# Masked attention with a residual: features in plain order, one store per quadrant, other slots for the blocks of batches five and six

## The chip, the cores and the metric

One core of a Trainium2 chip. The time is device microseconds of one execution, the median of several. Engines: PE (TensorE, matmul), DVE (VectorE), ACT (ScalarE), POOL (GpSimd) and SP (SyncE); SP, POOL and ACT also issue the transfers (DMAs), each through a queue of its own, and 16 DMA engines carry them out.

## What is computed

Eight batches of x, 512 features by 1024 tokens, float32, and a mask of zeros and ones with about half of the tokens kept. Queries, keys and values are one projection; 8 heads of 64 features.

```python
def reference(x, cond_2048, Wq, Wo):        # x (8, 512, 1024), mask (8, 1024), W (512, 512)
    q = transpose(x) @ Wq.T                  # split into 8 heads of 64
    scores = einsum('bhqd,bhkd->bhqk', qh, qh) / sqrt(64)
    logits = (scores * cmask + (1 - cmask) * -1e30) * rmask
    ctx = softmax(logits) @ qh               # heads joined again
    return x + transpose(ctx @ Wo.T)
```

A row whose token is masked has logits of zero throughout, so its attention is the mean of all values.

## The kernel before

Attention is computed for the kept tokens only (NK = 544 columns hold them, the last one the mean of x, which stands for every masked token). `early` runs before the number of kept tokens is known to the engines, `late` after a branch on it.

**Order of features.** A [128, 512] tile of x or of a weight has four features per partition or column group. Here partition p holds features 4p to 4p + 3: `load_piece` (L369) loads half a batch (512 tokens) as four transfers, one for each d, whose DRAM side has 128 rows with equal steps (L376). The rows of x that are written back to DRAM for the gather (`turn`, L399, stored by SP at L413; for batch 0 `turn_first`, L380) thus have columns in an order (a, d, f) other than the features'. `order_columns` (L926) and the wo branch of `turn_weights` (L938) bring the weights into it, `by_rows` and `as_rows` (L797) the last batch's results, and the stores at the end undo it.

**One batch** is four pairs of heads, and a pair five steps c = 0 to 4; `late` walks through 8 x 4 x 5 steps. In a step, PE computes scores (L610) and weighted values (L655), ACT the exponentials (L633). `project`, `turn_values` and `square` prepare the next pair. At a pair's step 0 `invert` (L727) turns the sums of the pair before: DVE writes rt, SP stores it in four small transfers (row, L736) and reads it back spread over partitions in two (rb, L741); at step 3 `contexts` (L756) uses rb on DVE (`sum_last`, L751). DVE works in order, so what stands behind a wait there, such as the copy of v (L545) that PE needs, waits too.

**Around it**, `plan` (L1087) puts tasks into steps by (batch, pair, step) with a rank. Tasks of rank below 5 come before `contexts`, the others behind it. For batch n: `load_piece` in batch n-2 at (0,1) and (0,2), the rows' transposes, the search for kept tokens on DVE, the gather on POOL (L474) and `collect`. For the results of batch b:

- `output` (L770): PE multiplies by wo (L780), ACT copies, POOL stores the rows into od (L793).
- `load_rows` (L846): SP loads 128 rows of x into a block g, 32 tokens of each quarter of the batch, in four transfers (L850). `firsts` has the steps.
- `fetch` (L888): POOL adds the results to g with an indirect transfer. `slots` has the steps.
- `finish_blocks` (L853): DVE transposes g into the buffer whole (L857), of which there is one. `ends` has the steps. After the last block (batches 0 to 4) or each fourth (5 and 6) a store is queued, which `issue_stores` (L910) issues at the end of the next step but one at most: 16 transfers on SP (L867), for each of four token quarters (a) and four feature groups (c).

Batch 7 has no pair after it to hide in. `begin_output` (L803) multiplies the first three pairs' part during the last pair, `end_output` adds the rest, `fetch_last` gathers by token, `finish_tokens` (L897) transposes back on PE, adds the x tile that still lies in SBUF, and ACT stores (L906).

SP, POOL and ACT issue transfers in program order; a transfer on SP waits for the one eight before it.

Of the kernel before, what the change touches and what calls it, by code (L numbers as in the profile page):

```python
# [10 lines left out]
F32 = mybir.dt.float32  # L11
# [10 lines left out]
Q = 32  # L22
# [283 lines left out]
def attention_of_kept_tokens(ctx, tc, x, mask, wq, wo, out, ident, wqT, woT, verdict, flag):  # L306


    nc = tc.nc
    B, D, T = x.shape  # L310
    P = 128
    DK = D // NH
    SCALE = 1.0 / math.sqrt(DK)
    ND = D // P
# [52 lines left out]
    stores = [[], []]  # L367

    def load_piece(b, r, queue=None):  # L369

        features = x[b].rearrange("(p d) t -> d p t", d=ND)
        if r == 0:
            xs[b] = []
        xs[b].append(sb.tile([P, ND, NB], F32, tag="x", name=f"x_{b}_{r}", bufs=NN))
        for d in range(ND):
            (queue or nc.sync).dma_start(  # L376
                xs[b][r][:, d, :], features[d][..., r * NB : (r + 1) * NB]
            )
# [417 lines left out]

    def by_rows(pr):  # L797
        return woT[:, pr, :].rearrange("p (a d f) -> p d a f", a=A, d=ND)

    def as_rows(t):  # L800
        return t.rearrange("p (d a f) -> p d a f", a=A, d=ND)

    def begin_output(b, i):  # L803

        n = sizes[i]
        po = bank(f"pa_{b}_{i}")
        for pr in range(ND - 1):
            nc.tensor.matmul(  # L808
                as_rows(po[:n, :]),
                cTs[b, pr][:, i * P : i * P + n],  # L810
                by_rows(pr),
                start=(pr == 0),
                stop=(pr == ND - 2),
            )
        pa = sb.tile([P, D], F32, tag="xin", name=f"pa_{b}_{i}", bufs=NC)
        note(nc.scalar.copy(pa[:n, :], po[:n, :]))
        partials[i] = pa

    def end_output(b, i, tag):
        n = sizes[i]  # L820
        od = place_outputs(b)
        po = bank(f"po_{b}_{i}", tag)
        nc.tensor.matmul(
            as_rows(po[:n, :]),
            cTs[b, ND - 1][:, i * P : i * P + n],
            by_rows(ND - 1),
            start=True,
            stop=True,
        )
# [12 lines left out]

    def by_blocks(t):
        return t.rearrange("(c f d) (a n) -> a f c d n", c=A, d=ND, a=A)

    def load_rows(b, i):  # L846
        g = sb.tile([P, D], F32, tag="g", name=f"g_{b}_{i}", bufs=NT)
        rows = rows_of_x[b][:T, :].rearrange("(a n) c -> a n c", a=A)
        for a in range(A):
            nc.sync.dma_start(g[a * Q : (a + 1) * Q, :], rows[a, i * Q : (i + 1) * Q, :])  # L850
        gs[b, i] = g

    def finish_blocks(b, i):  # L853
# [7 lines left out]
        if (i + 1) % n == 0:  # L861
            cols = slice((i + 1 - n) * Q, (i + 1) * Q)

            def store():
                for a in range(A):
                    for c in range(A):
                        nc.sync.dma_start(  # L867
                            by_blocks(out[b])[a][:, c, :, cols],
                            whole[a * Q : (a + 1) * Q, c * ND : (c + 1) * ND, cols],
                        )  # L870

# [25 lines left out]
    def finish_tokens(b, i):  # L897
# [4 lines left out]
        for d in range(ND):  # L902
# [3 lines left out]
        nc.scalar.dma_start(  # L906
            out[b, :, i * P : (i + 1) * P].rearrange("(p d) t -> p d t", d=ND), xr
        )
# [16 lines left out]

    def order_columns(w, nm):  # L926

        ws = []
        for e in range(ND):
            t = sb.tile([P, D], F32, tag="g", name=f"{nm}_in_order_{e}", bufs=NT)  # L930
            nc.scalar.copy(
                t.rearrange("p (a d f) -> p a d f", a=A, d=ND),
                w[e].rearrange("p (a f d) -> p a d f", a=A, d=ND),
            )
            ws.append(t)
        return ws

    def turn_weights(wT, nm, d, tag="t"):  # L938
        pt = bank(f"{nm}_t{d}", tag)
        for e in range(ND):  # L940
            nc.tensor.transpose(
                pt[:, e * P : (e + 1) * P], weights[nm][e][:, d * P : (d + 1) * P], ident
            )
        if nm == "wo":
            nc.scalar.copy(
                wT[:, d, :].rearrange("p (a d f) -> p a d f", a=A, d=ND),
                pt.rearrange("p (a f d) -> p a d f", a=A, d=ND),
            )
        else:
            nc.scalar.copy(wT[:, d, :], pt)  # L950

    def early():
# [64 lines left out]
        for r in range(NN):  # L1017
# [10 lines left out]
            nc.scalar.copy(searches[0][0][:, r * NB : (r + 1) * NB], pt)  # L1028
            if r == 0:
                for i in range(NT):  # L1030
                    turn_first(i)

# [15 lines left out]

        mean_first()
        for i in range(NC):  # L1050
            search(0, i)

    def count_blanks():
# [33 lines left out]
    def plan():  # L1087
# [62 lines left out]
        for b in range(B - 1):  # L1150
            nxt = b + 1
            if b < B - 3:
# [7 lines left out]
                firsts, slots = after[3:], after[6:]  # L1160
                ends = [(1, 4), (2, 0), (2, 1), (2, 4), (3, 0), (3, 0), (3, 1), (3, 4)]
                ends = [(nxt + 1, *at) for at in ends]
            elif b == B - 3:
                for i in range(LAST - 1):
                    put(nxt, i + 1, 3, output, b, i, 0, rank=6)
                    put(nxt, i + 1, 4, output, b, i, 1, rank=6)
                put(nxt, 3, 2, output, b, LAST - 1, 0, 1, rank=6)
                put(nxt, 3, 2, output, b, LAST, 0, 1, rank=6)
                firsts = [(nxt, 3, i) for i in range(NC)] + [(nxt + 1, 0, i) for i in range(NT - NC)]
                slots = [(nxt + 1, 0, (i + 1) // 2) for i in range(NT)]  # L1170
                ends = [(0, 3), (0, 4), (1, 0), (1, 1), (1, 1), (1, 2), (1, 4), (2, 0)]
                ends = [(nxt + 1, *at) for at in ends]
            else:
                put(nxt, 0, 4, output, b, 0, 0, 1, rank=6)
                put(nxt, 1, 2, output, b, LAST, 0, 1, rank=6)
                put(nxt, 1, 3, output, b, 1, 0, 1, rank=6)
                put(nxt, 1, 4, output, b, 2, 0, 1, rank=6)
                put(nxt, 2, 3, output, b, 3, 0, 1, rank=6)
# [22 lines left out]
    def late(n):  # L1201
# [176 lines left out]
```

## Time and profile before

| | |
|---|---|
| median of 3 runs | 764.5 us (753.38, 764.5, 764.69) |
| the profiled execution | 761.91 us |
| its span | 760.2 us |
| mean granted clock of PE | 0.929 |
| moved by DMA | 116.75 MB, 154 GB/s on average |

The span runs from the first to the last instruction of the profiled execution. In a line of the profile's timeline stand start, length (both us), engine, line of the kernel, operation and the tiles written and read, then how many instructions were merged; a bracket tells how long the engine had stood idle before and what ended that. SPq, POOLq and ACTq are those engines' issuing of transfers. In a line of the windows stand the stretch, its length, the busy time of PE, PEld (weight load), DVE, ACT and POOL, the clock, the DMA engines' busy share and GB/s.

### The profile page before, as it was taken

The page shows a single profiled execution, that of the slowest core. Times are in us where ns is not written, and L with a number is a line of the kernel's source. Part 1 is how long each engine was busy: PE and PEld are TensorE (multiplying, and loading weights), DVE is VectorE, ACT ScalarE, POOL GpSimd, SP SyncE. Part 2 cuts the span into 40 slices and gives each one's busy share as a digit, 9 for nine tenths or more (in the row PEclk, how much of TensorE's full clock was granted, in tenths as well). Part 3 has the DMA queues.
Part 4 walks back from the last instruction along what each step waited for, and adds up shares of the span by engine and source line. Part 5 has one row for each costly group of instructions (what it writes and reads, how often), then busy time and mean ns, then how long its engine had stood idle before and what let it go on. Part 6 is the DMA issues. An engine that isn't in the chain of part 4 may idle for free.

```text
span 760.2 us, 16407 instructions
## 1 busy us (share of the span) xinstructions
PE 650.5 (86%) x6187; PEld 368.8 (49%) x6187; DVE 347.8 (46%) x1044; ACT 375.1 (49%) x1048; POOL 183.1 (24%) x205
## 2 busy tenths in 40 slices
PE   5588899999999999799979997999999919989630
PEld 4454555555555554455535554555555505543220
DVE  7227566544545562455445552465445214332420
ACT  5365376666556654456535654655544504453000
POOL 4601302001243122412142121412241421133210
PEclk9788799999999999899989999999999968999855
DMA  8626535223677467863977387854773484455282
GB/s 279 219 63 191 154 95 170 72 88 92 207 167 183 106 184 211 180 166 105 273 171 165 91 234 207 187 143 124 195 159 88 108 199 111 130 126 97 93 259 49
DMA packets 100372, 116.75 MB, mean 154 GB/s; under 512 B 15488, under 2 KB 67200, under 8 KB 100272
## 3 DMA queue, kind: packets, MB, share of 16 engines
q1 hardware_dynamic: 79360, 74.09, 34.6%
q0 software_dynamic: 16688, 39.32, 22.3%
q10 hardware_dynamic: 4224, 2.10, 0.9%
q8 instruction: 52, 0.85, 0.5%
q14 instruction: 48, 0.39, 0.2%
HBM read 72.78 MB, written 42.67 MB: 152 GB/s over the span
## 4 chain that ended last, share of the span: by engine, by line
PE 51%; DMA 15%; SPq 14%; DVE 10%; issue 3%; ACT 3%; POOL 1%; POOLq 0%; DVEq 0%; ACTq 0%
PE pq L517 12%; PE s L610 11%; PE av L655 10%; PE po L780 8%; SPq L867 6%; SPq L850 4%; DMA rb<-row 4%; DMA g<-xd 4%; DMA row<-rt 3%; DMA x<-in_x_dram 3%; PE v L543 2%; PE pa L808 2%; DVE v L545 1%; SPq L741 1%; SPq L736 1%
## 5 line engine op out<-in xcount | busy, mean ns | idle before, releaser
L633 ACT ACTIVATE e<-s,bias 128x544 f32<-128x544 f32 x256 | 180.2, 709 | 107.7 <-PE s L610 107.5
L655 PE MATMUL av<-e,v 64*64 64x272 f32 x2048 | 152.8, 401 | 34.5 <-DVE v L545 34.3
L610 PE MATMUL s<-qT 64*64 64x272 f32 x2048 | 152.1, 410 | 0.0
L517 PE MATMUL pq<-xc,wqT 128*128 128x273 f32 (+1 forms) x512 | 138.1, 413 | 0.4 <-ACT wqT L950 0.4
L889 POOL DMA_INDIRECT g<-od,block_origin x56 | 88.4, 1578 | 144.4 <-DMA g<-xd 83.9
L655 PEld LDWEIGHTS av<-e,v 64*64 64x64 f32 x2048 | 79.8, 137 | 78.8 <-DVE v L545 38.5
L780 PE MATMUL po<-woT,cT 128*128 128x512 f32 (+1 forms) x448 | 115.9, 443 | 0.0
L517 PEld LDWEIGHTS pq<-xc,wqT 128*128 128x128 f32 x512 | 94.2, 194 | 43.8 <-issue 25.9
L610 PEld LDWEIGHTS s<-qT 64*64 64x64 f32 x2048 | 68.2, 135 | 69.7 <-issue 44.7
L793 POOL DMA_DIRECT2D od<-oc x56 | 30.7, 551 | 205.8 <-ACT oc L791 198.0
L474 POOL DMA_INDIRECT xin<-xd,source x40 | 38.0, 950 | 156.3 <-DMA row<-rt 42.8
L531 DVE COPY qm<-pq 128x1 f32<-128x1 f32 x32 | 5.1, 158 | 150.0 <-ACT qT L526 134.9
L780 PEld LDWEIGHTS po<-woT,cT 128*128 128x128 f32 (+1 forms) x448 | 48.3, 159 | 32.5 <-issue 31.7
L552 ACT ACTIVATE sq<-v 128x640 f32<-128x640 f32 x32 | 23.5, 736 | 59.3 <-DVE v L545 59.3
L545 DVE COPY v<-v 128x512 f32<-128x512 f32 x64 | 31.1, 487 | 47.2 <-PE v L543 47.2
L524 ACT COPY qT<-pq 128x272 f32<-128x272 f32 x64 | 24.7, 385 | 56.1 <-PE pq L517 56.1
L633 ACT ACTIVATION_READ_ACCUMULATOR e<-s,bias 128x1 f32 x256 | 50.1, 196 | 0.0
L857 DVE STREAM_TRANSPOSE whole<-g 128x512 f32<-128x512 f32 x56 | 38.0, 691 | 26.2 <-DMA g<-xd 16.2
L405 DVE STREAM_TRANSPOSE xt<-x 128x1024 f32<-128x1024 f32 x28 | 34.6, 1236 | 15.3 <-DMA x<-in_x_dram 14.6
L464 DVE TENSOR_SCALAR_CACHE_REDUCE junk<-rank,key 128x1024 f32<-128x1024 f32 (+4 forms) x40 | 39.9, 997 | 1.1 <-ACT rank L1028 1.1
L558 DVE TENSOR_REDUCE len<-sq 128x10 f32<-128x640 f32 x32 | 26.2, 820 | 27.3 <-ACT sq L552 27.3
L633 ACT ACTIVATE el<-s,bias 128x272 f32<-128x272 f32 x64 | 30.3, 478 | 12.5 <-PE s L624 12.3
(148 smaller groups left out, 605.0 us busy)
## 6 DMA issues: line engine op xcount, KB each, us to landing
x<-in_x_dram SPq DMA_DIRECT2D x56, 256.0 KB
xd<-xt SPq DMA_DIRECT2D x112, 128.0 KB
g<-xd SPq DMA_DIRECT2D x224, 64.0 KB
out_dram<-whole SPq DMA_DIRECT2D x80, 128.0 KB
rb<-row SPq DMA_DIRECT2D x60, 160.0 KB
od<-oc POOLq DMA_DIRECT2D x28, 256.0 KB, 2.5
out_dram<-whole SPq DMA_DIRECT2D x64, 64.0 KB
rank<-ranks SPq DMA_DIRECT2D x6, 512.0 KB
```

The source lines that it names most:

```text
L405: nc.vector.transpose(xt.rearrange("p k (d f) -> p k d f", d=ND), xs[b][r][:, :, at : at + n].rearrange("p d (k t) -> p k d t", t=Q),)
L464: nc.vector.tensor_scalar(junk[:, :n], rank[:, i * P :], key[:, col], 0.0, ALU.is_le, ALU.add, accum_out=found[:, col])
L474: nc.gpsimd.indirect_dma_start(out=xin[:n, :], out_offset=None, in_=rows_of_x[b], in_offset=bass.IndirectOffsetOnAxis(ap=searches[b][2][:n ...
L517: nc.tensor.matmul(pq[:, :n], wqT[:, d, pr * P : (pr + 1) * P], xcs[b][:, d, hf * KH : hf * KH + n], start=(d == 0), stop=(d == ND - 1),)
L545: nc.vector.tensor_copy(v[:, at : at + n, :], pt[:, : n * P].rearrange("p (c d) -> p c d", d=P))
L610: nc.tensor.matmul(s[h][to, hf, :KH], qT[heads[h], at : at + DK], qT[heads[h], hf * KH : (hf + 1) * KH], start=True, stop=True,)
L633: nc.scalar.activation(e[:, h], of[h], AF.Exp, bias=biases[pair][:, c : c + 1], scale=SCALE, accum_out=acc[:, h, c : c + 1],)
L655: mm = nc.tensor.matmul(avs[pair][hf][heads[h], :KH], v[rows, c, heads[h]], e[rows, h, hf, :] if c < LAST else e[rows, h, :], start=(c == ...
L780: nc.tensor.matmul(po[j * n : (j + 1) * n, :w], cTs[b, pr][:, i * P : i * P + n], woT[:, pr, j * w : (j + 1) * w], start=(pr == 0), stop=( ...
L857: nc.vector.transpose(whole[:, :, i * Q : (i + 1) * Q], gs.pop((b, i)).rearrange("p (k f) -> p k f", f=Q))
L867: nc.sync.dma_start(by_blocks(out[b])[a][:, c, :, cols], whole[a * Q : (a + 1) * Q, c * ND : (c + 1) * ND, cols],)
L889: nc.gpsimd.indirect_dma_start(out=gs[b, i], out_offset=None, in_=ods[b], in_offset=bass.IndirectOffsetOnAxis(ap=block_origin[:, b, i : i ...
```

## The change

Feature a·128 + d·32 + f now sits in partition a·32 + f under index d, so rows of x, weights and results have columns in the features' own order. `order_columns`, `by_rows`, `as_rows` and the wo branch go. A block's rows of x are loaded in one transfer, a quadrant (a) of results is stored in one. `finish_tokens` writes features d·128 + p, for which the last batch's x is loaded a second time (`load_again`, two transfers of 1 MB at steps 1 and 2 of that batch). At the start, `turn_first` comes behind both halves of the ranks and `mean_first` behind the search. In `plan`, the last end of batches 0 to 4 is three steps earlier; outputs, loads, fetches and ends of batches 5 and 6 (counted from 0) have other steps, and `begin_output` of the short last block moves behind the last pair's sums.

```diff
+    def load_again(b, r):
+        if r == 0:
+            xs[b] = []
+        xs[b].append(sb.tile([P, ND, NB], F32, tag="x", name=f"xe_{b}_{r}", bufs=NN))
+        nc.sync.dma_start(
+            xs[b][r], x[b, :, r * NB : (r + 1) * NB].rearrange("(d p) t -> p d t", d=ND)
+        )
...
-        features = x[b].rearrange("(p d) t -> d p t", d=ND)
+        features = x[b].rearrange("(a d f) t -> d a f t", a=A, d=ND)
...
-                as_rows(po[:n, :]),
+                po[:n, :],
-                by_rows(pr),
+                woT[:, pr, :],
...
-    def by_blocks(t):
-        return t.rearrange("(c f d) (a n) -> a f c d n", c=A, d=ND, a=A)
+    def in_blocks(t):
+        return t.rearrange("(k f) (a n) -> a f k n", f=Q, a=A)
...
         rows = rows_of_x[b][:T, :].rearrange("(a n) c -> a n c", a=A)
-        for a in range(A):
-            nc.sync.dma_start(g[a * Q : (a + 1) * Q, :], rows[a, i * Q : (i + 1) * Q, :])
+        nc.sync.dma_start(g, rows[:, i * Q : (i + 1) * Q, :])
...
                 for a in range(A):
-                    for c in range(A):
-                        nc.sync.dma_start(
-                            by_blocks(out[b])[a][:, c, :, cols],
-                            whole[a * Q : (a + 1) * Q, c * ND : (c + 1) * ND, cols],
-                        )
+                    nc.sync.dma_start(
+                        in_blocks(out[b])[a][:, :, cols], whole[a * Q : (a + 1) * Q, :, cols]
+                    )
...
-            out[b, :, i * P : (i + 1) * P].rearrange("(p d) t -> p d t", d=ND), xr
+            out[b, :, i * P : (i + 1) * P].rearrange("(d p) t -> p d t", d=ND), xr
...
-            if r == 0:
-                for i in range(NT):
-                    turn_first(i)
+        for i in range(NT):
+            turn_first(i)
...
-        mean_first()
         for i in range(NC):
             search(0, i)
+        mean_first()
...
-                ends = [(1, 4), (2, 0), (2, 1), (2, 4), (3, 0), (3, 0), (3, 1), (3, 4)]
+                ends = [(1, 4), (2, 0), (2, 1), (2, 4), (3, 0), (3, 0), (3, 1), (3, 1)]
...
-                firsts = [(nxt, 3, i) for i in range(NC)] + [(nxt + 1, 0, i) for i in range(NT - NC)]
-                slots = [(nxt + 1, 0, (i + 1) // 2) for i in range(NT)]
-                ends = [(0, 3), (0, 4), (1, 0), (1, 1), (1, 1), (1, 2), (1, 4), (2, 0)]
+                firsts = [(nxt, 2 + i // NC, i % NC) for i in range(2, 2 + NT)]
+                slots = [(nxt, 3, 4)] + [(nxt + 1, 0, i // 2) for i in range(NT - 1)]
+                ends = [(0, 2), (0, 2), (0, 4), (1, 0), (1, 1), (1, 1), (1, 2), (1, 4)]
...
-                slots = [(nxt, 2, 4)] + [(nxt, 3, (i + 1) // 2) for i in range(NT - 1)]
-                ends = [(nxt, 3, c) for c in (1, 2, 3, 4, 4)]
-                firsts = [(nxt, 1, 2), (nxt, 1, 3), (nxt, 1, 4), (nxt, 2, 0)]
-                firsts += [(nxt, 2, i) for i in range(4)]
+                firsts = [(nxt, 1 + i // NC, i % NC) for i in range(NT)]
+                slots = [(nxt, 2, 3), (nxt, 2, 4)] + [(nxt, 3, i // 2) for i in range(NT - 2)]
+                ends = [(nxt, 3, c) for c in (0, 1, 1, 2, 2, 4)]
...
         last = B - 1
-        for i in range(NC):
-            put(last, 3, (1, 2, 3, 4, 4)[i], begin_output, last, i, rank=7)
+        for r in range(NN):
+            put(last, 0, 1 + r, load_again, last, r)
+        for i in range(LAST):
+            put(last, 3, 1 + i, begin_output, last, i, rank=7)
...
-        weights["wq"] = order_columns(load_weights(wq, "wq"), "wq")
+        weights["wq"] = load_weights(wq, "wq")
...
         spread(last, inverses(last))
+        begin_output(B - 1, LAST)
         sum_last(last)
...
-        for i in range(5, NT):
+        for i in range(NT - 2, NT):
             finish_blocks(B - 2, i)
```

More of the change, by code (lines that the diff above doesn't have):

```diff
@@ L795, in attention_of_kept_tokens @@
     partials = {}
[L797 to L801, printed above, removed]
     def begin_output(b, i):
@@ L823, in end_output @@
         nc.tensor.matmul(
-            as_rows(po[:n, :]),
+            po[:n, :],
             cTs[b, ND - 1][:, i * P : i * P + n],
-            by_rows(ND - 1),
+            woT[:, ND - 1, :],
             start=True,
@@ L924, in load_weights @@
         return ws
[L926 to L936, printed above, removed]
     def turn_weights(wT, nm, d, tag="t"):
@@ L943, in turn_weights @@
             )
[L944 to L950, printed above, removed]
+        nc.scalar.copy(wT[:, d, :], pt)
     def early():
@@ L1160, in plan @@
                 firsts, slots = after[3:], after[6:]
[L1161 removed]
+                ends = [(1, 4), (2, 0), (2, 1), (2, 4), (3, 0), (3, 0), (3, 1), (3, 1)]
                 ends = [(nxt + 1, *at) for at in ends]
             elif b == B - 3:
[L1164 removed]
+                for i in range(2):
                     put(nxt, i + 1, 3, output, b, i, 0, rank=6)
                     put(nxt, i + 1, 4, output, b, i, 1, rank=6)
[L1167 to L1171 removed]
+                put(nxt, 3, 1, output, b, 2, 0, 1, rank=6)
+                put(nxt, 3, 2, output, b, 3, 0, 1, rank=6)
+                put(nxt, 3, 3, output, b, LAST, 0, 1, rank=6)
+                firsts = [(nxt, 2 + i // NC, i % NC) for i in range(2, 2 + NT)]
+                slots = [(nxt, 3, 4)] + [(nxt + 1, 0, i // 2) for i in range(NT - 1)]
+                ends = [(0, 2), (0, 2), (0, 4), (1, 0), (1, 1), (1, 1), (1, 2), (1, 4)]
                 ends = [(nxt + 1, *at) for at in ends]
```

6 lines of the change are left out of this document (3 added, 3 removed).

## The prediction

> **What bounds the kernel now.** I read the page first: span, engines and slices.
>
> ```profile
> span 760.2 us, 16407 instructions
> PE 650.5 (86%) x6187; PEld 368.8 (49%) x6187; DVE 347.8 (46%) x1044; ACT 375.1 (49%) x1048; POOL 183.1 (24%) x205
> PE   5588899999999999799979997999999919989630
> PE 51%; DMA 15%; SPq 14%; DVE 10%; issue 3%; ACT 3%; POOL 1%; POOLq 0%; DVEq 0%; ACTq 0%
> PE pq L517 12%; PE s L610 11%; PE av L655 10%; PE po L780 8%; SPq L867 6%; SPq L850 4%; DMA rb<-row 4%; DMA g<-xd 4%; DMA row<-rt 3%; DMA x<-in_x_dram 3%; PE v L543 2%; PE pa L808 2%; DVE v L545 1%; SPq L741 1%; SPq L736 1%
> ```
>
> PE is busy 86% of the time. The rest is in a few dips (the 7s, the 1 and the ends), and there the last two lines, the chain of waits, leave PE for SP's queue and its transfers: the result stores (L867), the rows of x (L850), the inverse sums (row, rb) and the x loads. So a transfer counts only where row and rb come late, at the start, and at the end.
>
> Next the timeline of SP, DVE and PE at the dips. The first six lines show what a batch costs; the next three the 1 of PE's slices; four more the end. The last line is from the DMA answer: what a fetch takes from issue to landing.
>
> ```profile
> 193.09 1.40 SPq L736 DMA_DIRECT2D row<-rt  x4
> 197.21 5.33 SPq L376 DMA_DIRECT2D x<-in_x_dram  x8
> 203.22 6.57 SPq L850 DMA_DIRECT2D g<-xd  x8
> 211.74 1.41 SPq L736 DMA_DIRECT2D row<-rt  x4
> 268.71 1.40 SPq L736 DMA_DIRECT2D row<-rt  x4
> 598.98 1.39 SPq L736 DMA_DIRECT2D row<-rt  x4
> ...
> 605.75 17.06 SPq L867 DMA_DIRECT2D out_dram<-whole  x16
> 625.37 0.71 DVE L857 STREAM_TRANSPOSE whole<-g 128x512 f32<-128x512 f32 x1 [16.21 <-DMA g<-xd]
> 628.47 2.09 PE L655 MATMUL av<-e,v 64*64 64x272 f32 x16 [16.97 <-DVE v L545]
> ...
> 699.77 5.53 PE L808 MATMUL pa<-woT,cT 128*128 128x512 f32 x12
> 709.98 6.48 PE L823 MATMUL po<-woT,cT 128*128 128x512 f32 x10 [2.36 <-DVE cT L694]
> 722.70 11.39 ACTq L906 DMA_DIRECT2D out_dram<-x  x8
> 717.59 32.23 SPq L867 DMA_DIRECT2D out_dram<-whole  x32
> ...
> g<-od,block_origin POOLq DMA_INDIRECT x56, 5.9
> ```
>
> The row transfers at 193.09, 268.71 and 598.98 open batches 2, 3 and 7. Batch 2 takes 75.6 us; batches 3 to 6 take 330.3, or 82.6 each: 4 x 7 = 28 us of stalls. These are the batches in which batch b-3's sixteen stores stand on SP just ahead of the x loads.
>
> **The change part by part.**
>
> *Issues and results.* A store is four transfers instead of sixteen, with the same packets, and batches 0 to 4 store three steps earlier. That takes the stores from in front of the x loads, so the 28 us can go. At 605.75 batch 4's store was still being issued when DVE wanted to write batch 5's first block into the same buffer; DVE waited 16.21 us, PE behind it 16.97. Now five steps lie between. What is late next there is the fetch of batch 5's second block, which DVE wants two steps (7.6 us) after the slot it is issued in, while a fetch takes 5.9 us and both `load_again` transfers run (2 MB on SP, ahead of the next row transfer, which is some four steps off). DVE waits 0 to 5 us, and the copy of v queued behind it holds PE. I take 3: 17 becomes 3, -14.
>
> *The end.* SP's last 32 stores run to 749.8; ACT's eight, which cannot be issued before their blocks are done, end at 734.1. Batch 6's first half now goes out in the last pair, its second half is four transfers: -15. `begin_output` of the short block moves into the 2.36 us in which PE waits for DVE (half of the 5.53 at 699.77): -2.4. In the last pair DVE now has two fetches and two blocks of 0.71 us ahead of `contexts`, where it had one: +1.4 (0 to 3). Sum -16.
>
> *Copies on ACT, order at the start.* The four copies that order wq go, wo's copy and the pa and po matmuls become contiguous: nothing, since PE waited for the gather and not for wq. `search` no longer waits for `turn_first`: nothing either if x is late (below).
>
> *The loads.* The x load's DRAM side was 128 equal steps; it is now (a, f), 4 by 32, per d. The g load's four transfers of 32 rows become one of (a, n), 4 by 32. How a transfer is dealt to the 16 DMA engines can be read from the DMA answer.
>
> ```profile
> q1 hardware_dynamic: 79360, 74.09, 34.6%
> x<-in_x_dram SPq DMA_DIRECT2D x56, 256.0 KB
> xd<-xt SPq DMA_DIRECT2D x112, 128.0 KB
> g<-xd SPq DMA_DIRECT2D x224, 64.0 KB
> out_dram<-whole SPq DMA_DIRECT2D x80, 128.0 KB
> rb<-row SPq DMA_DIRECT2D x60, 160.0 KB
> out_dram<-whole SPq DMA_DIRECT2D x64, 64.0 KB
> rank<-ranks SPq DMA_DIRECT2D x6, 512.0 KB
> row<-rt SPq DMA_DIRECT2D x120, 1.2 KB
> wq<-in_L_cond_Wq_dram SPq DMA_DIRECT2D x4, 256.0 KB
> od<-oc SPq DMA_DIRECT2D x4, 256.0 KB
> od<-oc SPq DMA_DIRECT2D x1, 64.0 KB
> mrow<-in_cond_dram SPq DMA_DIRECT2D x1, 32.0 KB
> ```
>
> These are all of q1's 732 transfers. The code gives each one's contiguous runs: 128 (x, wq, od, a whole store of 1 KB pieces, a half store of 512 B ones, rank), 256 (xd), 32 (g, short od), 64 (rb, mrow), 10 (row). Together 68,368. The queue had 79,360 packets, 10,992 more: exactly 16 for each of the 612 transfers whose outermost count is 32 or more, and 10 for each of the 120 of ten rows. So every engine that takes part adds one packet, and a ten-row transfer runs on ten engines: the outermost count sets the number. No transfer of before has 4 on one side and 128 on the other. It may get 16 engines or 4; I take 4, because an equal share must be cut from both sides, and the nearest row (ten for ten) shows no splitting below the outermost step.
>
> The Trainium skill ("DMA: Bandwidth & Descriptors", section "Why a DMA increments its semaphore by 16 and not by 1") says that a DMA gets the largest number of engines up to 16 that divides the slowest dimension of both its patterns, on the sync queue the lowest-numbered. By that these loads get four engines too and the sum stays as it is below; with sixteen it would be the first rival's. The ten packets for ten rows agree; four for 4 by 32 no run here shows.
>
> What four engines cost:
>
> ```profile
> 4.00:6.00 2.00, 1.93 (x9) 1.25 (x7) 0.28 (x1) 0.26 (x1) 0.29 (x1) 1.00 0.97 324
> 14.00:16.00 2.00, 0.00 (x0) 0.00 (x0) 1.50 (x4) 1.56 (x3) 0.83 (x3) 1.00 1.02 405
> 200.00:280.00 80.00, 78.81 (x832) 44.83 (x832) 45.02 (x133) 47.74 (x136) 23.08 (x22) 1.00 0.66 171
> 300.00:320.00 20.00, 14.67 (x103) 6.89 (x104) 8.04 (x25) 6.67 (x19) 8.36 (x7) 0.83 0.87 188
> 223.00 0.22 DVE L751 TENSOR_TENSOR rb<-rb 128x64 f32<-128x64 f32 x1
> 1.47 3.88 SPq L376 DMA_DIRECT2D x<-in_x_dram  x8
> 20.74 1.05 POOL L474 DMA_INDIRECT xin<-xd,source  x1 [3.89 <-DVE source L467]
> 214.64 1.09 SPq L741 DMA_DIRECT2D rb<-row  x2
> ```
>
> Windows end with clock, DMA share and GB/s. 324 / (16 x 0.97) is 20.9 GB/s for an engine, 405 / (16 x 1.02) 24.8. A 256 KB transfer on four engines then takes 3.1 or 2.6 us, eight x loads 25 or 21.
>
> Batch 2: x from 197.2 is through at 218 to 222, the two g loads behind it at 224 to 229, two or three later with the gathers that share the engines. The row issued at 211.74 stands behind them. From its last issue to rb's issue (213.15 to 214.64) is 1.5 us, rb's issue 1.1 and a landing like row's 1.5: 4.1 more, so 230 to 236 against 223.00, where DVE uses rb unheld now. Stall 7 to 13 us, with v, and so PE, queued behind `contexts`. After the stall at 302 to 308 the clock was 0.83 over 20 us: 2 to 3 us for a slow start. The five g loads behind rb (13 to 16 us) delay the next row by 0 to 3. That is 9 to 19. By load: a share of 0.66 of 80 us is 52.8 us an engine, of which x and g (16 x 256 KB) are 12.5 at 20.9 GB/s; on four engines that becomes 50, in all 90 in a batch of 75.6: +15 or more. I take 17 a batch, 9 to 24.
>
> Batches 2 to 5 have both loads: 4 x 17, batch 6 (g alone) +2, less the 28: +42 (9 to 72). Batches 0 and 1 have x alone: +5 (0 to 8). At the start the eight loads issued from 1.47 take 21 to 25 us where 2.1 MB at 324 GB/s took 6.5. Of these 15 to 19 us the gather at 20.74 hides 3.9: POOL stood idle that long for DVE's search, which is early now. +12 (8 to 15).
>
> Sum: 42 + 5 + 12 - 14 - 16 = +29. On the profiled execution's 761.91 us (the span and 1.7 around it), that is 791. The median of the three runs is 764.5, 2.6 above that execution; I leave the sum on the profile.
>
> **The rivals.**
>
> *The loads keep 16 engines* (faster). Then only gains stay: stalls 28 less some 6 for a store that now competes with the batch's last row, -14, -16, and -1 at the start: 761.9 - 53 = 709. For it: SBUF's side still counts 128. Against: the ten-row packets.
>
> *Four engines, but hidden* (faster). If row and rb do not wait behind x on the four engines, nothing new stalls: 761.9 - 28 - 14 - 16 + 12 = 716. For it: x is wanted only later. Against: today's stalls sit where row and rb follow x on the same queue.
>
> *Four engines, at the low price* (no change). At 9 us a batch the gains cancel the loss: 4 x 9 + 2 - 28 + 5 + 12 - 30 is -3, so 759. For it: the latency sum starts there. Against: the load sum asks 15 at least. It decides below 14 a batch, where the sum is +17, about the 2% line.
>
> **How the numbers follow.** About 2% can be told from no change here. Four engines with stalls: 0.83, own range 745 to 831 (all low ends, all high ends), of which 0.65 slower, 0.14 within, 0.04 faster. Sixteen engines: 0.12, hidden: 0.05, both faster. Faster 0.21, same 0.14, slower 0.65. The range 735 to 832 leaves out the two fast rivals and a little more.
>
> **What would show it.** q1's packets: by the same count 74,656 if x and g loads run on four engines, 76,000 if on sixteen. DMA share low while x loads run; PE's transposes at the start waiting for x till 23 or later; DVE's L751-step (rb) held 7 to 13 us in pair 1 of batches 2 to 5; no 17 us gap in batch 7; SP's last store before ACT's. It is wrong if x lands in 7 us at the start, or if rb is there when DVE asks.

## The result and the profile after

The changed kernel takes 848.02 us (median of 4 runs, 842.1 to 852.39) against 761.98 us before (4 runs, 753.38 to 764.69): a ratio of 1.1166, interval 1.1034 to 1.1298. Slower was forecast, but 791 us, with 832 as the upper end: the size is far off. The profiled execution of the changed kernel took 842.1 us, 80.2 more than that of before. Here and below a median is of all runs of a kernel, while a ratio and its interval are formed from the fast runs alone, so that it need not be the quotient of two medians shown.

The page of the profile after: span, engines, the slices of PE and DMA, the chain of waits, the sync queue and the group of PE that lost most.

```profile
span 840.3 us, 16009 instructions
PE 671.7 (80%) x6187; PEld 377.1 (45%) x6187; DVE 347.8 (41%) x1044; ACT 371.1 (44%) x1044; POOL 183.4 (22%) x205
PE   5389859979993989937996689939899999798753
DMA  3484433422344566365742657445664645856646
PE 50%; DMA 27%; DVE 11%; SPq 4%; issue 3%; ACT 3%; POOL 1%; DVEq 0%; POOLq 0%; ACTq 0%
DMA row<-rt 13%; PE pq L526 12%; PE av L664 11%; PE s L619 11%; PE po L789 9%; DMA rb<-row 7%; DMA x<-in_x_dram 4%; SPq L745 2%; PE v L552 2%; DVE cT L768 2%; DVE v L554 2%; PE pa L811 2%; SPq L385 1%; DVE rb L763 1%; PE top L581 1%
q1 hardware_dynamic: 74656, 76.16, 30.3%
L664 PE MATMUL av<-e,v 64*64 64x272 f32 x2048 | 158.9, 416 | 88.5 <-DVE v L554 87.7
```

The result stores and the issue of g, 10% of the chain before, are gone from it. In their place stand the small transfers row and rb, 20% where they had 7%. The last line shows what that costs PE: the weighted values stood idle for 88.5 us behind the copy of v, 34.5 before. In the list of waits it is DVE that holds this copy up:

```profile
DVE rb L760 <- DMA rb<-row: 102.8, 13, 16.6
```

102.8 us in 13 waits; before, the same wait came to 22.2 us in 7. The difference, 80.6 us, is DVE's, and not all of it reaches PE. Of the 80.1 us that the span grew, PE was idle for 58.9 (168.6 us against 109.7; 54.0 of the difference are the weighted values' wait for v). For the other 21.2 it was busy, with the same 6187 instructions, at a mean granted clock of 0.893 instead of 0.929.

The windows of the changed kernel, cut where a row transfer opens a batch (columns as before: stretch, length, five engines, clock, DMA share, GB/s):

```profile
0.00:75.01 75.01, 44.88 (x306) 31.75 (x307) 25.21 (x82) 28.00 (x69) 21.38 (x44) 0.83 0.52 146
75.01:143.40 68.39, 54.85 (x539) 33.29 (x543) 37.45 (x119) 35.31 (x102) 7.82 (x11) 0.84 0.43 121
143.40:225.72 82.32, 74.20 (x744) 41.66 (x740) 36.98 (x116) 44.33 (x128) 7.89 (x11) 0.94 0.32 95
225.72:322.70 96.98, 78.30 (x764) 43.34 (x760) 41.88 (x124) 45.01 (x129) 21.66 (x21) 0.91 0.56 149
322.70:420.82 98.12, 78.69 (x764) 43.42 (x760) 41.94 (x124) 44.99 (x129) 21.64 (x21) 0.90 0.57 152
...
618.32:703.30 84.98, 81.30 (x790) 45.71 (x783) 37.27 (x119) 42.06 (x118) 22.75 (x23) 0.98 0.54 140
703.30:840.30 137.00, 100.69 (x802) 51.37 (x801) 42.78 (x118) 41.40 (x115) 37.02 (x32) 0.85 0.60 153
```

Batch 2 before, for comparison with the fourth line:

```profile
193.09:268.71 75.62, 74.43 (x764) 42.13 (x760) 42.00 (x124) 45.22 (x129) 22.14 (x21) 1.00 0.65 167
```

PE is busy 3.9 us longer in this batch after the change, at a clock of 0.91 instead of 1.00, and the rest of the 21.4 us is idle time.

The same cuts in the kernels that follow, worked out from the starts of row transfers in their timelines (us; the start up to the first of them, which opens the second pair of batch 0, then the rest of batch 0 and batches 1 to 7):

| kernel | start | 0 | 1 | 2 | 3 | 4 | 5 | 6 | 7 | span |
|---|---|---|---|---|---|---|---|---|---|---|
| before | 60.0 | 59.9 | 73.2 | 75.6 | 84.1 | 83.7 | 82.9 | 79.6 | 161.2 | 760.2 |
| after | 75.0 | 68.4 | 82.3 | 97.0 | 98.1 | 98.8 | 98.7 | 85.0 | 137.0 | 840.3 |
| x16 | 60.7 | 57.2 | 74.8 | 86.9 | 85.6 | 85.4 | 84.5 | 86.4 | 136.9 | 758.4 |
| g16 | 74.2 | 68.0 | 82.0 | 88.5 | 88.1 | 90.4 | 88.2 | 82.8 | 133.4 | 795.7 |
| xg16 | 61.0 | 61.2 | 73.2 | 77.2 | 75.5 | 76.8 | 77.3 | 81.3 | 132.2 | 715.6 |
| b_g4 | 59.8 | 57.3 | 74.8 | 83.3 | 91.7 | 92.0 | 92.2 | 88.7 | 165.5 | 805.2 |
| b_g2 | 59.0 | 55.3 | 73.2 | 100.0 | 109.7 | 111.3 | 109.8 | 106.0 | 188.4 | 912.7 |
| b_slots | 59.8 | 61.4 | 74.8 | 77.8 | 75.9 | 75.9 | 78.1 | 81.0 | 136.8 | 721.5 |
| xg16_oldslots | 60.8 | 57.2 | 74.8 | 77.4 | 82.9 | 87.3 | 86.4 | 79.1 | 152.9 | 758.7 |
| g16_split | 74.2 | 67.7 | 73.2 | 91.4 | 91.2 | 92.4 | 89.9 | 83.4 | 132.0 | 795.3 |
| g16_early | 75.2 | 69.8 | 75.7 | 87.9 | 89.8 | 86.9 | 80.5 | 82.5 | 131.9 | 780.1 |

After against before: the start loses 15.0, batches 0 and 1 lose 17.6, batches 2 to 6 lose 71.7, batch 7 gains 24.2.

SP's timeline of batch 2 shows where its 21.4 us went, and two lines of DVE and one of PE what waited.

```profile
225.72 1.40 SPq L745 DMA_DIRECT2D row<-rt  x4
228.66 1.11 SPq L750 DMA_DIRECT2D rb<-row  x2
229.86 17.25 SPq L385 DMA_DIRECT2D x<-in_x_dram  x8
247.21 4.94 SPq L852 DMA_DIRECT2D g<-xd  x2
252.24 3.57 SPq L745 DMA_DIRECT2D row<-rt  x4
264.04 1.13 SPq L750 DMA_DIRECT2D rb<-row  x2
...
270.58 4.39 SPq L852 DMA_DIRECT2D g<-xd  x3
278.53 1.48 SPq L745 DMA_DIRECT2D row<-rt  x4
290.62 1.12 SPq L750 DMA_DIRECT2D rb<-row  x2
...
271.08 0.23 DVE L760 TENSOR_TENSOR rb<-rb 128x64 f32<-128x64 f32 x1 [15.37 <-DMA rb<-row]
296.30 0.23 DVE L760 TENSOR_TENSOR rb<-rb 128x64 f32<-128x64 f32 x1 [4.85 <-DMA rb<-row]
...
273.58 2.09 PE L664 MATMUL av<-e,v 64*64 64x272 f32 x16 [14.00 <-DVE v L554]
```

The eight x loads take SP 17.25 us to issue where they took 5.33. This is not the wait for the transfer eight before: the seventh of them follows rb, whose transfer had landed at 232.4, and its issue ran from 237.3 to 243.6. The issue itself lasts longer. At the start of the same kernel, where only the last of eight x loads has a transfer eight before it (the mask's, landed at 2.98), issuing one load takes up to 2.60 us (minimum, median and maximum in ns):

```profile
L385 SPq DMA_DIRECT2D x<-in_x_dram x8: 529/1536/2597, 1.5 to 11.6; - x8
```

Before it took 0.56 us at most. By the semaphore events of the trace, the issue of the fifth to the eighth load ended there at 6.43, 9.07, 11.60 and 14.16 us, and the load four before each had landed at 6.98, 9.62, 12.32 and 14.97. So SP gets some four of these loads ahead of the engines and then issues at their pace; what holds it there the trace does not name.

So row, wanted some 18.65 us after the row ahead of it (193.09 to 211.74 before), at 244.4, is issued at 252.24. Then it lies behind x and two g on the engines: rb, which reads it, can be issued at 264.04 only. DVE asks in vain for 15.37 us. One pair on, three g loads are enough for another 4.85. In each of batches 2 to 5 the two waits come to 19.9 to 21.0 us.

That x runs on four engines can be seen at the start of the same kernel, where little else moves:

```profile
10.00:12.00 2.00, 0.41 (x2) 0.01 (x1) 1.52 (x4) 0.41 (x1) 0.00 (x0) 1.00 0.26 99
26.00:28.00 2.00, 0.29 (x1) 0.00 (x0) 0.00 (x0) 0.00 (x0) 0.00 (x0) 0.50 0.26 100
```

A share of 0.26 is 4.2 of 16 engines, and 99 GB/s over four is 24.8 each, where all sixteen moved 324 in the same stage before. The semaphore events agree: besides one at the end of its issue, such a load has four landings, and a load of before has sixteen.

### The profile page after: what moved, and what is told of

Its sections match the earlier page's. It is cut to its first block, busy times and chain, and to the rows that moved or that the text cites. A ratio compares the mean times of both kernels' runs of the same rounds, so it can differ in the third digit from the quotient of the medians.

```text
span 840.3 us, 16009 instructions
## 1 busy us (share of the span) xinstructions
PE 671.7 (80%) x6187; PEld 377.1 (45%) x6187; DVE 347.8 (41%) x1044; ACT 371.1 (44%) x1044; POOL 183.4 (22%) x205
## 3 DMA queue, kind: packets, MB, share of 16 engines
q1 hardware_dynamic: 74656, 76.16, 30.3%
q0 software_dynamic: 18224, 39.33, 20.9%
## 4 chain that ended last, share of the span: by engine, by line
PE 50%; DMA 27%; DVE 11%; SPq 4%; issue 3%; ACT 3%; POOL 1%; DVEq 0%; POOLq 0%; ACTq 0%
DMA row<-rt 13%; PE pq L526 12%; PE av L664 11%; PE s L619 11%; PE po L789 9%; DMA rb<-row 7%; DMA x<-in_x_dram 4%; SPq L745 2%; PE v L552 2%; DVE cT L768 2%; DVE v L554 2%; PE pa L811 2%; SPq L385 1%; DVE rb L763 1%; PE top L581 1%
## 5 line engine op out<-in xcount | busy, mean ns | idle before, releaser
L664 PE MATMUL av<-e,v 64*64 64x272 f32 x2048 | 158.9, 416 | 88.5 <-DVE v L554 87.7
L789 PE MATMUL po<-woT,cT 128*128 128x512 f32 (+1 forms) x448 | 122.7, 460 | 0.0
L561 ACT ACTIVATE sq<-v 128x640 f32<-128x640 f32 x32 | 23.6, 736 | 126.5 <-DVE v L554 126.4
L789 PEld LDWEIGHTS po<-woT,cT 128*128 128x128 f32 (+1 forms) x448 | 51.2, 166 | 35.2 <-issue 34.9
L760 DVE TENSOR_TENSOR rb<-rb 128x64 f32<-128x64 f32 x32 | 7.1, 220 | 108.5 <-DMA rb<-row 102.8
L496 PE MATMUL xc<-ident,xin 128*128 128x128 f32 (+1 forms) x160 | 25.3, 284 | 22.4 <-DVE v L554 14.8
```

The lines of the kernel that those rows point to most:

```text
L664: mm = nc.tensor.matmul(avs[pair][hf][heads[h], :KH], v[rows, c, heads[h]], e[rows, h, hf, :] if c < LAST else e[rows, h, :], start=(c == ...
L789: nc.tensor.matmul(po[j * n : (j + 1) * n, :w], cTs[b, pr][:, i * P : i * P + n], woT[:, pr, j * w : (j + 1) * w], start=(pr == 0), stop=( ...
```

## The experiments

### One load at a time back on sixteen engines: x16, g16, xg16

x16 cuts the x load by a instead of by d. It stays four transfers of 256 KB per half, now 32 partitions by four features by 512 tokens.

```diff
-        features = x[b].rearrange("(a d f) t -> d a f t", a=A, d=ND)
+        features = x[b].rearrange("(a d f) t -> a f d t", a=A, d=ND)
-        for d in range(ND):
+        for a in range(A):
             (queue or nc.sync).dma_start(
-                xs[b][r][:, d, :], features[d][..., r * NB : (r + 1) * NB]
+                xs[b][r][a * Q : (a + 1) * Q, :, :], features[a][..., r * NB : (r + 1) * NB]
             )
```

> The changed kernel with the x loads cut by a instead of d: four transfers per half as before, each with 32 outermost steps on both sides. Theory (outermost count 4 means four of the sixteen DMA engines, and row and rb wait behind x): q1 packets 75,328; while x loads at the start the DMA share is near 1 instead of 0.26; the 15 us waits of DVE for rb in pair 1 of batches 2 to 5 go, the 5 us ones of pair 2 (g) stay; start, batches 0 and 1 back by 14, 8 and 9 us; in all some 848 - 31 - 60 = 757 us. Rival (the loss is in the rest: order at the start, slots, merged stores, the second load of x): 840 to 848 us.

Measured: 766.05 us, ratio to before 1.0077 (1.0041 to 1.0113). q1 has 75,328 packets. The start and batches 0 and 1 are back at 60.7, 57.2 and 74.8; batches 2 to 5 take 84.5 to 86.9 us, since g still runs on four engines, and the waits for rb fall from 102.8 to 38.8 us. The 9 us above the expectation are these batches: I had counted g's share as 5 us of each, and against the 75.6 us of batch 2 before it is about 10.

g16 gives the g load back its four transfers of 32 rows.

```diff
-        nc.sync.dma_start(g, rows[:, i * Q : (i + 1) * Q, :])
+        for a in range(A):
+            nc.sync.dma_start(g[a * Q : (a + 1) * Q, :], rows[a, i * Q : (i + 1) * Q, :])
```

> The changed kernel with the g load as four transfers of 32 rows again, x left on four outermost steps. Theory: q1 packets 78,016; the 5 us waits for rb in pair 2 of batches 2 to 5 go and batch 6 loses its 9, the 15 us ones of pair 1 stay or shrink by a few us since only two g transfers stand behind x there: 848 - 20 - 9 - some 10 in batch 7 = 809 us. Rival (x alone holds the queue, g is hidden): 840 to 848 us. Rival (issue of 168 more transfers costs): above 848.

Measured: 797.62 us, ratio 1.0464 (1.0398 to 1.053), 78,016 packets; 69.1 us of waits for rb are left. 50.4 us less than the changed kernel, more than the 39 expected. Issuing 168 more transfers costs nothing that shows.

xg16 is both edits together.

> Both together: every x and g load has 32 outermost steps. Theory: q1 packets 78,688, no wait for rb over 5 us in batches 0 to 5, and the gains of slots and stores alone are left: about 711 us (the prediction's first rival, on the median). Rival (the change costs elsewhere too): 735 us or more, and if nothing else in it gains, 764.

Measured: 721.55 us, ratio 0.9508 (0.942 to 0.9595). Its page:

```profile
span 715.6 us, 16282 instructions
PE 645.5 (90%) x6187; PEld 370.1 (52%) x6187; DVE 347.1 (49%) x1044; ACT 372.2 (52%) x1044; POOL 183.8 (26%) x205
q1 hardware_dynamic: 78688, 76.18, 40.9%
L664 PE MATMUL av<-e,v 64*64 64x272 f32 x2048 | 151.2, 398 | 11.0 <-DVE v L554 10.1
```

The idle time of the weighted values goes from 88.5 to 11.0 us, and the same kernel that lost 86 us gains 39. Nothing but the shape of two loads differs: same bytes, same queue, same steps, same arithmetic. The loss of the change is the two loads' outermost count. They nearly add up: putting x right takes 82.0 us off, g 50.4, both 126.5.

### The same fault put into the kernel before: b_g4, b_g2

b_g4 is the kernel before with the g load in one transfer, the edit of g16 the other way round.

> The kernel before with nothing but its g load joined into one transfer of 4 by 32 rows. Theory: q1 packets 76,000; batches 2 to 6 wait for rb behind g on four engines, 5 to 10 us each: 762 + 25 to 50 = 787 to 812 us. Rival (fewer transfers to issue is what counts, the four engines are hidden): 750 to 764 us.

Measured: 805.64 us, ratio 1.055 (1.0464 to 1.0636), 76,000 packets. One load of one line, with three quarters fewer transfers to issue, and the kernel is 5.5% slower. The rival by which fewer transfers are better falls.

b_g2 takes two transfers of 2 by 32 rows:

```diff
-        for a in range(A):
-            nc.sync.dma_start(g[a * Q : (a + 1) * Q, :], rows[a, i * Q : (i + 1) * Q, :])
+        for a in range(0, A, 2):
+            nc.sync.dma_start(g[a * Q : (a + 2) * Q, :], rows[a : a + 2, i * Q : (i + 1) * Q, :])
```

> The kernel before with its g load as two transfers of 2 by 32 rows. Theory (an outermost count of k means k engines): q1 packets 76,000 as with one transfer of 4 by 32, two engines at a time and the same two, so 2.1 MB of g take some 42 us of each batch instead of 21; batches 2 to 6 go from some 92 us to 104 to 112, in all 865 to 905 us. Rival (a short outermost count is slow in itself, whatever it is): 800 to 815 us. Rival (two transfers spread over four engines): 800 to 815 us as well, with packets 76,000.

Measured: 914.59 us (one run), batches 2 to 6 at 100 to 111 us; a little beyond the expectation, far beyond both rivals. Two windows in which g is nearly all that moves, and the queue:

```profile
240.00:242.00 2.00, 2.00 (x13) 0.66 (x11) 0.00 (x0) 0.40 (x2) 0.09 (x1) 1.00 0.13 50
242.00:244.00 2.00, 0.38 (x8) 0.00 (x0) 0.00 (x0) 0.00 (x0) 1.51 (x1) 1.00 0.14 52
...
q1 hardware_dynamic: 76000, 74.08, 27.1%
```

0.13 of 16 is two engines, and 50 GB/s is 25 for each: half of what 4 by 32 gets. Several of these transfers were in flight then (six issued from 225.54 to 240.33), and together they still had two engines: the same two for each.

### What the rest of the change is worth: b_slots, xg16_oldslots, xg16_ends

b_slots is the kernel before with the changed plan alone (outputs, loads, fetches and ends, and begin_output of the short block): features in the old order, sixteen transfers per store. The core of it:

```diff
-                ends = [(1, 4), (2, 0), (2, 1), (2, 4), (3, 0), (3, 0), (3, 1), (3, 4)]
+                ends = [(1, 4), (2, 0), (2, 1), (2, 4), (3, 0), (3, 0), (3, 1), (3, 1)]
...
-                firsts = [(nxt, 3, i) for i in range(NC)] + [(nxt + 1, 0, i) for i in range(NT - NC)]
-                slots = [(nxt + 1, 0, (i + 1) // 2) for i in range(NT)]
-                ends = [(0, 3), (0, 4), (1, 0), (1, 1), (1, 1), (1, 2), (1, 4), (2, 0)]
+                firsts = [(nxt, 2 + i // NC, i % NC) for i in range(2, 2 + NT)]
+                slots = [(nxt, 3, 4)] + [(nxt + 1, 0, i // 2) for i in range(NT - 1)]
+                ends = [(0, 2), (0, 2), (0, 4), (1, 0), (1, 1), (1, 1), (1, 2), (1, 4)]
...
```

> The kernel before (order of features, 16 transfers per store, four per block of rows) with the changed plan alone: steps of outputs, loads, fetches and ends, and begin_output of the short block. Theory (the slots carry the gain): batches 3 to 6 lose some 20 of their 28 us, the 17 us gap in batch 7 falls under 8, the tail keeps 16 transfers of its half store: 720 to 735 us. Rival (joining the store's transfers carries it; sixteen transfers three steps earlier only hold another row): 748 to 765 us.

Measured: 716.55 us, ratio 0.9388 (0.9314 to 0.9461), the lowest median of all kernels here, though its interval overlaps those of xg16, xg16_ends and xg16_alt. Batches 3 to 5 take 75.9 to 78.1 us where they took 82.9 to 84.1. xg16_oldslots is the complement: xg16 with the plan of before.

> The kernel xg16 with the plan of before (and its begin_output): joined stores, loads on sixteen engines, old steps. Theory (the slots carry the gain): 745 to 760 us, since the store still stands ahead of the x loads and in the way of the next block. Rival (the joined stores carry it): 718 to 732 us, near xg16's 721.55.

Measured: 756.39 us, ratio 0.9962 (0.9922 to 1.0002). Its PE line at the place of the old 17 us gap, and SP at the start of batch 3:

```profile
637.35 2.09 PE L664 MATMUL av<-e,v 64*64 64x272 f32 x16 [19.02 <-DVE v L554]
...
274.37 4.92 SPq L869 DMA_DIRECT2D out_dram<-whole  x4
279.34 8.75 SPq L385 DMA_DIRECT2D x<-in_x_dram  x8
```

The store is issued in 4.92 us instead of 10.90, and still the gap and the long batches (82.9 to 87.3) remain: it is the step at which the store stands that matters, not the number of its transfers (for batches 3 to 5 the plan moves nothing else). The plan is worth some 43 us in the old order of features (759.18 less 716.55) and some 35 in the new one (756.39 less 721.55, from two sets of runs). How its parts share this was not tested. Plain order and joined stores, given sixteen engines, show no gain: 0.9962 without the new plan, and with it 721.55 against 716.55, whose intervals overlap.

xg16_ends moves the first three ends of batch 5 to (0, 3), (0, 4), (0, 4).

> The kernel xg16 with the first three blocks of batch 5 turned one or two steps later ((0,3), (0,4), (0,4) instead of (0,2), (0,2), (0,4)). Theory (in batch 7 DVE waits 7.7 us for fetched blocks there, and PE 6.6 us behind it): 721.55 - 4 to 7 = 715 to 718 us. Rival (the wait moves with it, since POOL issues the eight fetches back to back until 600 us): 720 to 724 us.

Measured: 718.86 us, ratio 0.9433 (0.9379 to 0.9487), against 0.9508 (0.942 to 0.9595) for xg16. The intervals overlap: whether anything is gained is open.

### Place or load: g16_split, g16_early

With g on sixteen engines and x on four, does x cost time because of what stands behind it, or because four engines have too much to do? Both kernels move the x loads of batches 3 to 7 and nothing else. First g16_split:

```diff
-                    loads = [(b, 0, 1), (b, 0, 2)]
+                    loads = [(b, 0, 1), (b, 1, 1)]
```

> The kernel g16 (x still 4 by 32, on four engines by the count) with the second half's x load of batches 3 to 7 moved from step 2 of the first pair to step 1 of the second, so that a half (1 MB, some 10.5 us at 100 GB/s) lies between two row transfers some 18 us apart. Theory (a load on four engines costs only what row and rb wait behind it): the 7 to 11 us waits for rb in batches 1 to 5 fall under 3 us, these batches to 75 to 80 us: 797.6 - 5 x 8 to 11 = 745 to 758 us; start and batch 0 stay slow. Rival (the four engines are loaded beyond what a batch leaves, wherever the loads stand): 785 to 798 us.

Measured: 800.25 us, ratio 1.0524 (1.0456 to 1.0592): nothing gained. Batch 1 fell from 82.0 to 73.2, as expected; batches 2 to 5 stayed at 90 to 92. SP in the second pair of batch 2, and DVE one pair later:

```profile
244.00 2.69 SPq L385 DMA_DIRECT2D x<-in_x_dram  x4
246.81 5.49 SPq L853 DMA_DIRECT2D g<-xd  x4
252.41 9.21 SPq L422 DMA_DIRECT2D xd<-xt  x4
261.73 5.63 SPq L853 DMA_DIRECT2D g<-xd  x12
267.45 1.87 SPq L745 DMA_DIRECT2D row<-rt  x4
272.43 1.14 SPq L750 DMA_DIRECT2D rb<-row  x2
...
279.42 0.22 DVE L760 TENSOR_TENSOR rb<-rb 128x64 f32<-128x64 f32 x1 [14.11 <-DMA rb<-row]
```

The wait of the second pair went, and one of 14.11 us came in the third: four xd stores took 9.21 us to issue behind the moved x loads, the row came late behind them. So this run moved the jam and decides nothing. Then g16_early:

```diff
-                    loads = [(b, 0, 1), (b, 0, 2)]
+                    loads = [(b - 1, 3, 1), (b, 0, 1)]
```

> The kernel g16 (x still 4 by 32) with the first half's x load of batches 3 to 7 moved one pair earlier (step 1 of the last pair of the batch before) and the second half's to step 1 of the first pair: each half has a row transfer only after some 18 us and few g loads behind it, which the run g16_split did not give. Theory of place (what counts is what of the small transfers stands behind x): batches 2 to 5 fall from 88 to 90 us to 77 to 80, in all 797.6 - 8 - 40 = 750 us. Theory of load (in xg16 an engine is busy 0.78 of 76 us, 59 us, of which x is 5.3; on four engines x is 21.1, so these four need 75 of 76 us, wherever it stands): batches 2 to 5 stay at 86 to 91 us, in all 785 to 798 us.

Measured: 781.01 us, ratio 1.0246 (1.0171 to 1.0322). Batch 1, with two halves of x and no g, takes 75.7; batches 2 to 4, with two halves and g, 86.9 to 89.8; batch 5, with one half, 80.5. The place alone is refuted as the cause (750 was expected of it): where g, the gathers and the fetches run too, two halves of x on four engines cost 10 to 14 us against xg16 in batches 2 to 4, even at this place. The total also lies below the 785 to 798 us of the theory of load. But my account of a full load was too neat. The load of xg16 is not as fast as I took it to be (at the end), so x is more than 5.3 us of an engine's 59 there, and four engines need less than the 75 of 76 us that I wrote. A share of 0.62 in the 88.00 us from 224.00 to 312.00 of g16 is 54.6 us an engine, of which x, evenly spread, is 5.3; with its 21.1 on four engines these have some 70 of 88. They are the most loaded, not full, and how much of the wait is queueing behind single transfers stays open.

```profile
224.00:312.00 88.00, 76.38 (x756) 42.49 (x749) 41.50 (x120) 44.62 (x129) 21.66 (x21) 0.94 0.62 162
```

## Why the prediction was wrong

**Four engines: right.** The count of packets told 74,656 from 76,000, and it is 74,656. Every kernel's count came out as computed (75,328, 78,016, 78,688, 76,000 twice), and the windows show the rate. The rule that the prediction cites from the Trainium skill ("DMA: Bandwidth & Descriptors", section "Why a DMA increments its semaphore by 16 and not by 1") is now shown for two cases for which there was no run then: 4 by 32 runs on four engines, 2 by 32 on two, at about 25 GB/s each.

**Middle batches: the term that was mis-sized.** 17 us a batch and 2 for batch 6, less 28, made +42 (9 to 72); +71.7 was measured, the end of its range. Against 75.6 us, batches 2 to 5 stalled for 21.4 to 23.2. The step that failed in it is the issue of x on SP: the reckoning of the row's path took it for what it had been, 5.33 us, and only the engines for slow. It took 17.25 us, since SP itself went at the pace of the four engines, so the row was not even issued in time, and rb, put at 37 to 43 us after the batch's first row, was used at 45.4 (225.72 to 271.08). The next pair was given 0 to 3 us, with 4.85 measured, and the slow start 2 to 3, where PE was busy 3.9 us longer. The second estimate, by load, set the busy time of an 80 us window against a batch of 75.6; over 75.6 us the same sum gives 87 us, so +12 and not +15. What was measured lies above the 19 of the first estimate and near the 24 of the range; 17 was a middle. The 28 us to be gained also counted batch 6, which has no x load: it took 79.6 us before and takes 81.3 in xg16, so its 4 us were not there to gain, and of its 9.4 over 75.6 after the change only 3.7 are g's.

**Batches 0 and 1: the step that failed.** They were priced at 5 (0 to 8) with no working but that x stands there alone, without g; 17.6 was measured. x alone holds up the row behind it too: in batch 1 the loads are issued until 163.6, and rb, which reads that row, can be issued at 175.6 only. In batch 0 DVE waits 8.4 us for rb in the same way.

```profile
147.01 16.63 SPq L385 DMA_DIRECT2D x<-in_x_dram  x8
163.74 3.65 SPq L745 DMA_DIRECT2D row<-rt  x4
175.60 1.14 SPq L750 DMA_DIRECT2D rb<-row  x2
...
179.46 0.23 DVE L760 TENSOR_TENSOR rb<-rb 128x64 f32<-128x64 f32 x1 [6.90 <-DMA rb<-row]
```

**Start: right.** +12 (8 to 15) was forecast, +15.0 measured; the last transposes wait for x until 28.43.

**Batch 7 and the end: right in kind.** -14 and -16 make -30; xg16 shows -29.0, the changed kernel -24.2, because its g loads are on four engines there too. The 17 us gap became 6.06; for the wait that takes its place I had 3 (0 to 5), behind fetches that run beside `load_again`. In xg16, with all loads fast, PE waits 6.6 us there, so the four engines alone are not the cause; in b_slots, with the same plan and no `load_again`, it waits 2.4 us at most, so the plan alone is not either. By the semaphore events the first two fetches take 6.6 and 8.4 us to land in xg16, beside `load_again`, and 4.4 and 5.5 us in b_slots: that is the mechanism of the forecast, at a higher price. In the changed kernel they take 4.9 and 5.7, but the first is issued 6.1 us after the batch's first row instead of 2.0, once the last results stored into od have landed (at 708.0):

```profile
718.37 2.09 PE L664 MATMUL av<-e,v 64*64 64x272 f32 x16 [6.06 <-DVE v L554]
```

**The sum and the range.** The misses are 30 in the middle, 13 in batches 0 and 1, 3 at the start and 6 in batch 7: about 51, and the sum was 29 where 80.1 came. All have one sign, and most have one cause (row and rb late behind loads on four engines), so they do not average out. The range was built from bounds on each term, and the bound of 8 for batches 0 and 1 left out that a row transfer waits there as well.

**The rivals.** "Sixteen engines" was wrong of this kernel but near as a forecast of the repaired one: 709 on the profiled execution, 717.2 in xg16's. The 8 between them are a middle that gained 17.8 instead of 22 (batches 2 to 6), the start and batch 0, which lost 2.3 where 1 was to be gained, and 1 in batch 7. "Hidden" and "low price" (9 us a batch) fall with 102.8 us of waits for rb and 21 to 23 us lost in each of batches 2 to 5. Where I credited the gain to fewer transfers in a store as well as to its place, b_slots and xg16_oldslots show that the plan alone is enough for all of it.

## What to carry to other kernels

Rewriting an access so that it becomes one neat transfer can cost most of the DMA engines: look at the outermost count on both sides. Here 32 and 128 gave sixteen engines, 4 gave four and 2 gave two, and four transfers on sixteen engines beat one on four. When a load slows down, price not its own wait but that of the smallest urgent transfer behind it on the same queue, and add the time by which the issue itself lasts longer when the engines cannot take what is issued (17.25 us here, where it was 5.33). A change that moves slots and layout at once should be tried in halves: here one half alone gains 6% (716.55 us), and the other on top of it costs 18% (848.02).

## What the runs showed of the hardware that was not expected

A load that uses all sixteen engines can still be slow. At the same place of the start, x16 moved 217 and 206 GB/s with the engines wholly busy; the load of before, whose transfers write 128 partitions instead of 32, moved 324. Pieces of 2 KB are the same in both. b_x32 puts the cut by partitions alone into the kernel before:

```diff
-        features = x[b].rearrange("(p d) t -> d p t", d=ND)
+        features = x[b].rearrange("(p d) t -> p d t", d=ND)
-        for d in range(ND):
+        for a in range(A):
+            rows = slice(a * Q, (a + 1) * Q)
             (queue or nc.sync).dma_start(
-                xs[b][r][:, d, :], features[d][..., r * NB : (r + 1) * NB]
+                xs[b][r][rows, :, :], features[rows, :, r * NB : (r + 1) * NB]
             )
```

> The kernel before with its x load cut into four transfers of 32 partitions by four features by 512 tokens instead of four of 128 partitions by 512 tokens: same bytes, same 2 KB pieces, same features in the same places, sixteen engines by the count (q1 packets 79,360 as before). Theory (32 partitions of SBUF take only so much, as x16 showed with 217 GB/s): 205 to 225 GB/s in the windows 4 to 6 and 6 to 8 us instead of 324 and 328, the start 2 to 4 us longer, and in all 0 to 15 us slower, 762 to 775 us. Rival (x16's rate came from its order of features in DRAM, 32 rows apart within a transfer): 320 GB/s and 754 to 764 us.

Measured: 769.65 us, ratio 1.0107 (1.0034 to 1.018), 79,360 packets as before. Its windows at the start:

```profile
4.00:6.00 2.00, 1.93 (x9) 1.24 (x7) 0.28 (x1) 0.26 (x1) 0.27 (x1) 1.00 1.01 210
6.00:8.00 2.00, 1.98 (x9) 1.68 (x8) 1.72 (x14) 0.00 (x0) 0.48 (x1) 1.00 1.10 208
```

Each feature has its partition of before, and the rate is x16's: that points to the 32 partitions. One more thing differs, in b_x32 as in x16: a transfer reads 128 adjacent rows of DRAM, where one of before read every fourth of 512. In xg16 adjacent rows alone are not slow. By its semaphore events the eight x loads of the start land 1.2 us apart, and the four loads of wq right behind them, of 256 KB too, from 128 adjacent rows but into 128 partitions, 0.6 us apart. (The rows of wq also follow one another without a gap, so this is not the same pattern.) The engines show as busy while they move two thirds. The Trainium skill ("SBUF — State Buffer", section "Door 1: The DMA port swizzle (why `[64,N]` ≈ `[32,N]`)") says that 32 partitions from 0 on reach 8 of 16 ports, and gives about 218 GB/s as the limit for them; the 206 to 217 GB/s of x16 and b_x32 agree. By the same section partitions 64 to 127 have the other ports. xg16_alt therefore issues the four transfers of xg16 in the order of a = 0, 2, 1, 3 instead of 0, 1, 2, 3.

> The kernel xg16 with its four x transfers of a half issued in the order of a = 0, 2, 1, 3. Theory by the Trainium skill (SBUF - State Buffer, the DMA port swizzle: partitions 0 to 63 reach one half of the ports, 64 to 127 the other), if neighbouring transfers overlap: 240 to 320 GB/s at 4 to 8 us instead of 221 and 206, and 2 to 6 us less in all. Rival, from xg16's windows alone (each transfer is through before the next begins, so their order does not matter): 205 to 225 GB/s and 717 to 726 us.

Measured: 718.24 us, ratio 0.943 (0.934 to 0.9519), not to be told from xg16's 0.9508 (0.942 to 0.9595). In the windows:

```profile
4.00:6.00 2.00, 1.93 (x9) 1.22 (x8) 0.33 (x2) 0.26 (x1) 0.23 (x1) 1.00 1.05 243
6.00:8.00 2.00, 2.00 (x10) 2.00 (x11) 1.67 (x14) 0.00 (x0) 0.53 (x1) 1.00 1.07 229
```

243 and 229 GB/s where xg16 had 221 and 206: neighbouring transfers overlap a little, far from the 324.

POOL's own queue counted 18,224 packets in every kernel that loads x as 4 by 32 (after, g16, g16_split, g16_early) and 16,688 in the others. Eight x loads, those of batch 1, go through POOL, so this is 192 more for each of them, where SP's count fell by 12 for each of its own. Their time from issue to landing was 10.8 us against 5.6 before. Why this queue adds packets where the other drops them is open.
